# A context tile that arrives already turned, by single-element loads, and tiled matmuls kept together in the plan

## The chip, the core and the metric

The kernel runs on one core of one Trainium2 chip. The metric is the device time of one execution in microseconds. The core has five engines that work from their own instruction queues, each strictly in the order of its queue: PE (TensorE, matrix products and transposes), DVE (VectorE), ACT (ScalarE), POOL (GpSimd) and SP (SyncE, which here only issues transfers). Sixteen DMA engines move the data that SP's and ACT's queues ask for.

## What is computed

Sixteen sequences go through two layers, all in float32. Cut to what matters here, for each sequence `x[b]` (256 tokens of 256 channels), its context `ctx[b]` (256 tokens of 256 channels) and its condition:

```
# layer 0
nx = layer_norm(x) * gamma + beta
scores = (nx @ Wq) @ (ctx @ Wk).T / 16          # 256 x 256
evidence = softmax(scores) @ (ctx @ Wv)
routed = sum over 3 experts of softmax(router)[e] * (silu([nx, evidence, cond] @ e_w1[e]) @ e_w2[e])
x = x + sigmoid(gate) * (routed @ out_w + out_b)
# layer 1: shift, scale and gate of each part come from silu(cond) @ w_ada
x = x + g1 * self_attention(ln(x))               # 16 heads, windows of 128 tokens
x = x + g2 * topk_cross_attention(ln(x), ctx)    # keys and values from ctx, the 16 best of 256 per row
x = x + g3 * swiglu(ln(x))                       # 256 -> 2 x 1024 -> 256
```

So the context is used in three places: as the right side of the evidence scores (channels on the partitions), as the values of the evidence (tokens on the partitions), and as the source of the cross-attention's keys and values (channels on the partitions).

## The kernel before

The kernel is written as a list of small works, and a planner at build time decides the order of the instructions. A work is a generator that yields operations (`Op`): an engine, a cost in microseconds, the buffers that it reads, writes, takes and frees, and a function that emits the instructions. `Flow.run` is a list scheduler: among all operations whose inputs are planned, it takes the one that could begin first by the planner's own costs (`t_mm`, `t_tr`, `t_dve`, `t_act`, `t_pool`; ties and near ties are settled by a rank), emits its instructions, and moves on. The result is one fixed order for each engine. Waits on the chip are set afterwards from the true data dependences between the instructions, not from the plan's times.

`STAGES` lists the stages of a sequence with a rank, the buffers to keep free, a window and the stages that it must follow with a lag in sequences: `evidence` (layer 0 up to the router), `experts`, `self_keys`, `self`, `self_out`, `queries`, `keys`, `cross`, `cross_out`, `inputs`, `mlp`. Several sequences are in work at once, each in another stage.

The tiles that the change touches:

- A sequence's context is loaded as `cx` with tokens on the partitions, by one load of 128 x 2 rows of 1 KB on SP's queue (`sequence`, through the helper `load`, L426).
- `evidence` turns it: `chunks_T` makes four TensorE transposes of 128x128 into a PSUM bank (L484), and `copied` brings the bank to SBUF on ACT or DVE (L518, L520). The turned tile is `cT`.
- `cT` is the right side of the evidence scores (`by_token`, L567), and later the source of `cross_keys`. The planner is told of it as an input of `cross_keys`; for the evidence scores only `qT` is named as an input.
- TensorE works in three ways here: the whole array, `tiled="rows"` (head scores with 16 channels in a strip of 32 rows, L1368 and L1499) and `tiled="columns"` (the weighted sums of heads, L1288, and the router, L1094). The planner charges `TURN` = 0.093 us when the way changes.
- The scaling of the attention weights by GpSimd is `scale` in `self_attention` (L1408), planned with 1.02 us for four pieces.

Of the kernel before, what the change touches and what calls it, by code (L numbers as in the profile page):

```python
# [15 lines left out]
P = 128  # L16
# [20 lines left out]
PE, DVE, ACT, POOL, SP = range(5)  # L37
# [25 lines left out]


def t_pool(cols, n=1):
    return n * (0.03 + cols * 0.00237)


class Buf:
# [26 lines left out]
class Op:  # L96
# [5 lines left out]

    def __init__(
        self, engine, us, trace, r=(), w=(), new=(), free=(), table=None, size=0, tiled=None,
        other=(), grain=0.0,
    ):
        self.grain = grain
        self.tiled = tiled
        self.ways = ((engine, us, trace), *other)
        self.engine, self.us, self.trace, self.table, self.size = engine, us, trace, table, size  # L110
        self.tail = 0.0
        self.r, self.w, self.free = tuple(r), tuple(w), tuple(free)
        self.out = tuple(Buf(ring) for ring in new)
        self.done, self.end = False, 0.0
        self.after = ()
# [10 lines left out]
class Flow:  # L126
# [4 lines left out]
    ASIDE = 1.0  # L131
    TURN = 0.093
    SWITCH = 3.0
    RATE = 0.31e6
    LAND = 1.7

# [95 lines left out]
    def run(self):  # L232
        while self.works:
            moved = False
            for w in tuple(self.works):
                moved |= self.advance(w)
            self.works = [w for w in self.works if w.posted or not w.ended]
            best = None
            for w in self.works:
                wanted = set()  # L240
                for op in w.posted:
                    at = self.start(w, op, wanted)
                    wanted.update(b.ring for b in op.out)
                    if at is None:
                        continue
                    begin = max(self.now[op.engine], at)
                    late = 0.0
                    if op.table and op.table != self.table:
                        late = max(0.0, self.SWITCH - (begin - at))
                    key = (begin + late, at + w.rank + late)  # L250
                    if best is None or key < best[0]:
                        best = (key, w, op, at)
            if best is None:
                if not moved and self.works:
                    raise RuntimeError("no work can go on")
                continue
            _, w, op, at = best
            us = op.us
            begin = max(self.now[op.engine], at)
            if op.table and op.table != self.table:  # L260
                self.table = op.table
                us += self.LOAD
            if op.engine == PE:
                if op.tiled != self.tiled or op.tiled == "rows":
                    us += self.TURN
                self.tiled = op.tiled
            end = begin + us
            if op.grain and op.engine in self.port:
                self.port[op.engine] = begin, end, op.grain
            if op.size:  # L270
                self.moved = max(self.moved, end) + op.size / self.RATE
                op.tail = self.moved + self.LAND - end
            for b in op.out:
                b.ring.take(b)
            op.trace(*(b.t for b in op.out))
            op.done, op.end = True, end + op.tail
            w.posted.remove(op)
            self.now[op.engine] = end
            self.busy[op.engine] += us
            self.log.append((begin, end, op.engine, op.trace))  # L280
            for b in op.out + op.w:
                b.ready, b.by = end + op.tail, op.engine
            for b in op.r + op.w + op.out:
                b.read, b.last = max(b.read, end + op.tail), op.engine
            for b in op.free:
                b.ring.free.append((max(b.read, b.ready) + 0.15, b.slot))
# [3 lines left out]
def pixart_kernel(  # L290
# [9 lines left out]
    nc = tc.nc  # L300
# [63 lines left out]
    units = Ring(tiles(first, FIRST, [P, 2, T], "u"))  # L364
# [45 lines left out]
    flow = Flow()  # L410
# [68 lines left out]
    def chunks_T(src, free=True, ts=ALL):  # L479

        def trace(pt):
            for c in range(2):
                for t in ts:
                    nc.tensor.transpose(  # L484
                        pt[:, c, t * P : (t + 1) * P], src.t[:, t, c * P : (c + 1) * P], ident
                    )
        return (
            yield from make(
                PE, t_tr(2 * len(ts)), trace, r=(src,), new=(banks,),
                free=(src,) if free else (),  # L490
            )
        )
# [22 lines left out]
    def copied(pt):  # L515
        return (
            yield from make(
                ACT, t_copy(512), lambda u: nc.scalar.copy(u, pt.t),  # L518
                r=(pt,), new=(units,), free=(pt,),
                other=((DVE, t_dve(512), lambda u: nc.vector.tensor_copy(u, pt.t)),),  # L520
            )
        )
# [505 lines left out]
    def sequence(b, s):  # L1028
# [11 lines left out]
            3,  # L1040
        )

    def evidence(b, s):
        if "cx" not in s:
            yield from sequence(b, s)
        cx, xb = s["cx"], s["x"]
        pt = yield from chunks_T(cx, free=False)
        cT = s["cT"] = yield from copied(pt)
        xn = yield from normed(xb, 1e-5)
        pt = yield from chunks_T(xn)  # L1050
        nx = yield from by_chunk(
# [8 lines left out]
            r=(sc,), new=(smalls,),  # L1060
        )

        def exps(u):
# [5 lines left out]
        ex = yield from make(  # L1069
            ACT, 0.92, exps, r=(sc,), w=(am,), new=(units,), free=(sc,),  # L1070
            table="exp",
        )
# [231 lines left out]
    def self_weigh(t, v, exs, oT, ended):  # L1304

        pTs = []
        for j in range(4):
            while len(exs) <= j:
                yield None

            def turn(pt, j=j):
                for i in range(4):
                    nc.tensor.transpose(heads4(pt)[:, i, :], heads4(exs[j].t)[:, i, :], ident)  # L1313
            pt = yield from make(PE, t_tr(4), turn, r=(exs[j],), new=(banks,), free=(exs[j],))
            pT = yield from copied(pt)
            pTs.append(pT)

        def sum_up(to):
            for c in range(2):
                for a in range(2):  # L1320
                    for j in range(4):
                        h = 8 * c + 2 * j + a
                        weigh(
                            flat(to), h, c, v.t[:, t, h, :], heads4(pTs[j].t)[:, 2 * c + a, :],
                            a == 0, a == 1,
                        )
        pm = yield from make(
            PE, 1.01, sum_up, r=(v, *pTs), new=(banks,), free=tuple(pTs), tiled="columns",
        )
        yield Op(  # L1330
            ACT, t_copy(256),
            lambda: nc.scalar.copy(
                oT.t[:, :, t * P : (t + 1) * P],
                pm.t[:, 0, :].rearrange("p (c n) -> p c n", c=2),
            ),
            r=(pm,), w=(oT,), free=(pm,),
            other=((DVE, t_dve(256), lambda: nc.vector.tensor_copy(
                oT.t[:, :, t * P : (t + 1) * P],
                pm.t[:, 0, :].rearrange("p (c n) -> p c n", c=2),
            )),),  # L1340
        )
        ended.append(t)
# [15 lines left out]
    def self_attention(b, s, ts):  # L1358
        qT, kM, v = s["self"]
        oT, _, ended = yield from heads(s, v, ts)  # L1360
        for t in ts:
# [19 lines left out]
            for j in range(4):  # L1381
# [23 lines left out]
                def scale(ex=ex, nm=nm):  # L1405
                    for i in range(4):
# [1 line left out]
                        nc.gpsimd.tensor_scalar(  # L1408
                            part, part, nm.t[:, 8 + i : 9 + i], 1.0, ALU.mult, ALU.mult
                        )  # L1410
                yield Op(POOL, 1.02, scale, r=(nm,), w=(ex,), free=(nm,), grain=0.255)
                exs.append(ex)

    def self_output(b, s, ts):
# [8 lines left out]
    def cross_weigh(c, t, v, exs, lefts, oT, ended):  # L1423

        pTs = []
        for j in range(4):
# [3 lines left out]
            def mask_out(s, j=j):  # L1430
# [12 lines left out]
                w=(sm,),  # L1443
# [21 lines left out]
        def sum_up(to):  # L1465
# [7 lines left out]
                        )  # L1473
        pm = yield from make(
            PE, 1.01, sum_up, r=(v, *pTs), new=(banks,), free=tuple(pTs), tiled="columns",
        )
        yield Op(
            ACT, t_copy(128),
# [98 lines left out]
    def mlp(b, s, ts):  # L1577
# [36 lines left out]


    STAGES = (
        ("self_keys", self_keys, 5.0, 2, 2, 4, (("experts", 0), ("self", 1), ("cross", 3))),
        ("evidence", evidence, 5.0, 9, 0, 4, (("experts", 2),)),
        ("self", self_attention, 0.0, 4, 0, 12, (("self_keys", 0), ("cross", 3))),
        ("queries", cross_queries, 3.0, 1, 0, 32, (("self_out", 0), ("cross", 1))),  # L1620
        ("mlp", mlp, 8.0, 4, 0, 6, (("inputs", 0),)),
        ("cross_out", cross_output, 1.0, 1, 0, 8, (("cross", 0),)),
        ("cross", cross_attention, 4.0, 2, 1, 24, (("queries", 0), ("keys", 0))),
        ("experts", experts, 7.0, 3, 0, 8, (("evidence", 0), ("self_out", 3))),
        ("inputs", mlp_inputs, 8.0, 6, 1, 32, (("cross_out", 0), ("queries", 0))),
        ("keys", cross_keys, 6.0, 6, 2, 10, (("evidence", 0), ("cross", 1))),
        ("self_out", self_output, 5.0, 1, 0, 16, (("self", 0),)),
    )
    NEEDS = {
        "self_keys": ("wqkv", "mod"), "self_out": ("wso", "gates"),  # L1630
# [83 lines left out]
```

## Time and profile before

| | us |
|---|---|
| median of 3 runs | 1782.67 (1780.29 to 1784.48) |
| the profiled execution, its own time | 1784.01 |
| its span, first to last instruction | 1782.2 |
| PE busy | 1748.2 (98%) |
| DVE busy | 1406.4 (79%) |
| ACT busy | 1156.4 (65%) |
| POOL busy | 805.5 (45%) |
| transfers of the SP queue, share of 16 DMA engines | 7.8% |

An entry in the profile's groups names the line, the engine, the operation and the tiles (output first, buffer numbers left out), then the count, the busy time, the mean duration and the idle time before it. TensorE's durations overlap, because products are pipelined: a step from start to start is shorter than the duration of one. In float32 each product is run as two passes, so its count in the profile is twice that in the program. DMA rows give the share of 16 engines' time that packets took.

### The profile page before, as it was taken

The numbers are of one execution on the slowest core, as the hardware profiler recorded it, in microseconds if no ns is written. First come the engines' busy times: TensorE is split into PE (matmuls) and PEld (weight loads), VectorE is DVE, ScalarE is ACT, GpSimd is POOL, SyncE is SP. The second block draws the span as 40 slices with busy tenths as digits, with TensorE's granted clock in tenths as the row PEclk, the third lists the DMA queues.
The fourth block names the chain that finished last, engine by engine and source line by source line (L and its number), as shares of the span: only waits on it lengthen the run. The fifth ranks groups of instructions, "written<-read, shape, count | busy, mean of one in ns | idle before, by whom it ended". The sixth has DMA issues, their size and how long they took to land.

```text
span 1782.2 us, 36821 instructions
## 1 busy us (share of the span) xinstructions
PE 1748.2 (98%) x12105; PEld 1416.4 (79%) x12105; DVE 1406.4 (79%) x5637; ACT 1156.4 (65%) x3008; POOL 805.5 (45%) x1809
## 2 busy tenths in 40 slices
PE   8999999999999999999999999999999999999998
PEld 5687878788888788877878787878878787878888
DVE  2223878979988796979899996987986887989982
ACT  3246677776667668585666768577675757685651
POOL 1123355545454545445354554554363635364341
PEclk9999999999999999999999999999999999999999
DMA  8300000000000000000000000000000000010101
GB/s 294 120 18 1 10 16 13 8 13 19 13 19 7 25 13 19 7 25 7 19 13 14 19 8 25 13 15 5 13 19 7 13 19 13 13 37 10 28 31 30
DMA packets 33802, 45.12 MB, mean 25 GB/s; under 512 B 5609, under 2 KB 23579, under 8 KB 33099
## 3 DMA queue, kind: packets, MB, share of 16 engines
q1 hardware_dynamic: 33611, 42.77, 7.8%
q8 instruction: 96, 1.57, 0.4%
q14 instruction: 95, 0.78, 0.1%
HBM read 38.46 MB, written 4.30 MB: 24 GB/s over the span
## 4 chain that ended last, share of the span: by engine, by line
PE 65%; DVE 25%; ACT 4%; issue 2%; POOL 2%; DMA 1%; SPq 0%; POOLq 0%; DVEq 0%; ACTq 0%
PE bank L556 28%; PE bank L567 17%; DVE u L1526 5%; DVE small L1522 4%; PE bank L1457 4%; PE bank L1288 4%; DVE u L1564 3%; DVE small L1557 3%; DVE u L1433 3%; PE bank L1313 3%; PE bank L1499 2%; PE bank L484 2%; PE bank L1368 2%; PE bank L721 1%; ACT u L1393 1%
## 5 line engine op out<-in xcount | busy, mean ns | idle before, releaser
L1449 POOL TENSOR_SCALAR u<-u,small 128x256 f32<-128x256 f32 x512 | 255.2, 514 | 316.8 <-DVE small L1442 281.1
L556 PE MATMUL bank<-u,w 128*128 128x256 f32 x1536 | 360.7, 381 | 0.1
L518 ACT COPY u<-bank 128x512 f32<-128x512 f32 x389 | 222.9, 603 | 190.8 <-PE bank L1457 110.3
L556 PEld LDWEIGHTS bank<-u,w 128*128 128x128 f32 x1536 | 286.2, 191 | 44.2 <-issue 7.4
L1545 ACT ACTIVATE u<-bank,small 128x256 f32<-128x256 f32 x512 | 213.7, 480 | 99.0 <-DVE u L1526 60.7
L556 PE MATMUL bank<-u,wm 128*128 128x256 f32 (+1 forms) x1088 | 248.4, 371 | 3.6 <-ACT u L498 1.9
L1408 POOL TENSOR_SCALAR u<-u,small 128x128 f32<-128x128 f32 x512 | 184.8, 385 | 106.3 <-DVE small L1403 91.3
L1522 DVE MAX8 small<-bank 128x8 f32<-128x256 f32 x512 | 192.6, 418 | 42.4 <-PE bank L1499 42.3
L556 PEld LDWEIGHTS bank<-u,wm 128*128 128x128 f32 x1088 | 189.6, 191 | 35.3 <-issue 6.1
L1526 DVE MATCH_REPLACE8 u<-small,bank 128x256 f32<-128x256 f32 x512 | 208.4, 415 | 0.0
L1433 DVE SCALAR_TENSOR_TENSOR u<-u,u 128x256 f32<-128x256 f32 x512 | 207.6, 446 | 0.0
L1564 DVE MATCH_REPLACE8 u<-small,u 128x256 f32<-128x256 f32 x512 | 205.6, 410 | 0.0
L1557 DVE MAX8 small<-u 128x8 f32<-128x256 f32 x512 | 188.3, 412 | 0.0
L567 PE MATMUL bank<-w,u 128*128 128x256 f32 x768 | 184.3, 383 | 3.8 <-ACT u L498 3.8
L1393 ACT ACTIVATE u<-bank,small 128x128 f32<-128x128 f32 x512 | 180.2, 416 | 10.0 <-DVE small L1384 9.8
L567 PEld LDWEIGHTS bank<-w,u 128*128 128x128 f32 x768 | 142.9, 191 | 25.8 <-ACT u L498 4.9
L1536 POOL TENSOR_SCALAR small<-small 128x2 f32<-128x2 f32 x256 | 55.0, 216 | 222.8 <-DVE small L1522 181.2
L1457 PE MATMUL bank<-ident,u 128*128 128x128 f32 x1024 | 149.9, 276 | 3.9 <-ACT u L498 2.1
L1457 PEld LDWEIGHTS bank<-ident,u 128*128 128x128 f32 x1024 | 121.7, 142 | 35.2 <-POOL u L1449 8.9
L1393 ACT ACTIVATION_READ_ACCUMULATOR u<-bank,small 128x1 f32 x512 | 130.4, 256 | 0.0
L1384 DVE TENSOR_REDUCE small<-bank 128x4 f32<-128x512 f32 x128 | 79.5, 683 | 56.3 <-PE bank L1368 56.2
L596 POOL TENSOR_TENSOR u<-u,u 128x256 f32<-128x256 f32 x96 | 69.8, 748 | 118.1 <-DVE u L588 91.7
(172 smaller groups left out, 3109.0 us busy)
## 6 DMA issues: line engine op xcount, KB each, us to landing
u<-gates_d SPq DMA_DIRECT2D x51, 256.0 KB
u<-in_ctx_dram SPq DMA_DIRECT2D x16, 256.0 KB
w<-in_L_xcond_e_w_dram SPq DMA_DIRECT2D x3, 1024.0 KB
wada<-in_L_xcond_w_ada_dram SPq DMA_DIRECT2D x1, 2304.0 KB
u<-in_x_dram SPq DMA_DIRECT2D x16, 128.0 KB
u<-in_x_dram SPq DMA_DIRECT2D x32, 64.0 KB
wm<-in_L_xcond_w_m_dram SPq DMA_DIRECT2D x1, 2048.0 KB
out_dram<-u SPq DMA_DIRECT2D x16, 128.0 KB
```

The source lines that it names most:

```text
L518: ACT, t_copy(512), lambda u: nc.scalar.copy(u, pt.t),
L556: nc.tensor.matmul(to[:, c, cols(ts)], lhsT=w[:, k, col + c * P : col + (c + 1) * P], rhs=rhs[k // 2].t[:, k % 2, cols(ts)], start=start, ...
L567: nc.tensor.matmul(to[:, t, :], lhsT=lhs[k // 2].t[:, k % 2, t * P : (t + 1) * P], rhs=w(k), start=start, stop=stop,)
L1393: nc.scalar.activation(heads4(u)[:, i, :], heads4(sc.t)[:, i, :], AF.Exp, bias=nm.t[:, i : i + 1], accum_out=nm.t[:, 4 + i : 5 + i],)
L1433: nc.vector.scalar_tensor_tensor(ex[:, a, :], left[:, a, :], TAKEN, ex[:, a, :], ALU.is_equal, ALU.mult, accum_out=s[:, a : a + 1],)
L1449: nc.gpsimd.tensor_scalar(ex, ex, sm.t[:, 2 + a : 3 + a], 1.0, ALU.mult, ALU.mult)
L1457: nc.tensor.transpose(heads4(pt)[:, 2 * a + k, :], exs[j].t[:, a, k * P : (k + 1) * P], ident,)
L1522: nc.vector.max(m8s[j].t[:, 16 * a : 16 * a + 8], sc.t[:, a, :])
L1526: nc.vector.match_replace(firsts[j].t[:, a, :], m8s[j].t[:, 16 * a : 16 * a + 8], sc.t[:, a, :], TAKEN,)
L1545: nc.scalar.activation(u[:, a, :], sc.t[:, a, :], AF.Exp, bias=nm.t[:, a : a + 1])
L1557: nc.vector.max(m8s[j].t[:, 16 * a + 8 : 16 * a + 16], firsts[j].t[:, a, :])
L1564: nc.vector.match_replace(left, m8s[j].t[:, 16 * a + 8 : 16 * a + 16], left, TAKEN)
```

## The change

From the fourth sequence on, a new stage `context` loads the context a second time, with channels on the partitions, straight from DRAM into a tile. It does so by two loads on ACT's queue, one for each half of the channels; partition `p` gets the 256 values `context[b, 0:256, p]`, which lie 1 KB apart in DRAM, so every element is a piece of its own. `evidence` then leaves out the four transposes and the copy. The load with tokens on the partitions stays, since the evidence values need it. The planner counts the operation as 0.2 us of ACT, and its tile as ready 60 us later.

In the planner, `TURN` is charged only between the whole array and either tiled way (before: at any change of way, and at every row-tiled operation). A tiled operation that follows a tiled one is preferred by `STAY` = 2.0 in rank, and the two weighted sums are held back by `HOLD` = 1.0 in rank while the array is whole. GpSimd's costs are raised, and the order of the stages, some ranks, windows and buffers to keep are others.

```diff
 def t_pool(cols, n=1):
-    return n * (0.03 + cols * 0.00237)
+    return n * (0.03 + cols * 0.0027)
...
+    STAY = 2.0
+    HOLD = 1.0
...
-                    key = (begin + late, at + w.rank + late)
+                    rank = w.rank
+                    if op.engine == PE:
+                        if self.tiled is None:
+                            rank += op.hold
+                        elif op.tiled:
+                            rank -= self.STAY
+                    key = (begin + late, at + rank + late)
...
             if op.engine == PE:
-                if op.tiled != self.tiled or op.tiled == "rows":
+                if (op.tiled is None) != (self.tiled is None):
                     us += self.TURN
...
+    def turned_context(b, s):
+
+        if "cx" in s:
+            return
+
+        def trace(t):
+            for c in range(2):
+                nc.scalar.dma_start(
+                    out=t[:, c, :], in_=context[b].rearrange("k (c p) -> c p k", p=P)[c]
+                )
+        op = Op(ACT, 0.2, trace, new=(units,))
+        op.tail = 60.0
+        yield op
+        s["cT"] = op.out[0]
+
     def evidence(b, s):
...
-        pt = yield from chunks_T(cx, free=False)
-        cT = s["cT"] = yield from copied(pt)
+        if "cT" not in s:
+            pt = yield from chunks_T(cx, free=False)
+            s["cT"] = yield from copied(pt)
+        cT = s["cT"]
...
             PE, 1.01, sum_up, r=(v, *pTs), new=(banks,), free=tuple(pTs), tiled="columns",
+            hold=flow.HOLD,
...
-                yield Op(POOL, 1.02, scale, r=(nm,), w=(ex,), free=(nm,), grain=0.255)
+                yield Op(POOL, 1.42, scale, r=(nm,), w=(ex,), free=(nm,), grain=0.355)
...
     STAGES = (
+        ("context", turned_context, 0.0, 8, 0, 4, (("evidence", 1), ("experts", 2))),
         ("self_keys", self_keys, 5.0, 2, 2, 4, (("experts", 0), ("self", 1), ("cross", 3))),
-        ("evidence", evidence, 5.0, 9, 0, 4, (("experts", 2),)),
-        ("self", self_attention, 0.0, 4, 0, 12, (("self_keys", 0), ("cross", 3))),
-        ("queries", cross_queries, 3.0, 1, 0, 32, (("self_out", 0), ("cross", 1))),
+        ("self_out", self_output, 5.0, 1, 1, 16, (("self", 0),)),
+        ("experts", experts, 7.0, 3, 0, 8, (("evidence", 0), ("self_out", 3))),
+        ("queries", cross_queries, 3.0, 1, 0, 4, (("self_out", 0), ("cross", 1))),
...
-        ("inputs", mlp_inputs, 8.0, 6, 1, 32, (("cross_out", 0), ("queries", 0))),
-        ("keys", cross_keys, 6.0, 6, 2, 10, (("evidence", 0), ("cross", 1))),
-        ("self_out", self_output, 5.0, 1, 0, 16, (("self", 0),)),
+        ("self", self_attention, 0.0, 4, 0, 12, (("self_keys", 0), ("cross", 3))),
+        ("inputs", mlp_inputs, 8.0, 8, 1, 24, (("cross_out", 0), ("queries", 0))),
+        ("keys", cross_keys, 4.0, 6, 2, 10, (("evidence", 0), ("cross", 1))),
+        ("evidence", evidence, 5.0, 11, 0, 4, (("experts", 2), ("context", 0))),
     )
```

More of the change, by code (lines that the diff above doesn't have):

```diff
@@ L104, in __init__ @@
         self, engine, us, trace, r=(), w=(), new=(), free=(), table=None, size=0, tiled=None,
-        other=(), grain=0.0,
+        other=(), grain=0.0, hold=0.0,
     ):
+        self.hold = hold
         self.grain = grain
@@ L1475, in cross_weigh @@
             PE, 1.01, sum_up, r=(v, *pTs), new=(banks,), free=tuple(pTs), tiled="columns",
+            hold=flow.HOLD,
         )
@@ L1623, in pixart_kernel @@
         ("cross", cross_attention, 4.0, 2, 1, 24, (("queries", 0), ("keys", 0))),
-        ("experts", experts, 7.0, 3, 0, 8, (("evidence", 0), ("self_out", 3))),
-        ("inputs", mlp_inputs, 8.0, 6, 1, 32, (("cross_out", 0), ("queries", 0))),
-        ("keys", cross_keys, 6.0, 6, 2, 10, (("evidence", 0), ("cross", 1))),
-        ("self_out", self_output, 5.0, 1, 0, 16, (("self", 0),)),
+        ("self", self_attention, 0.0, 4, 0, 12, (("self_keys", 0), ("cross", 3))),
+        ("inputs", mlp_inputs, 8.0, 8, 1, 24, (("cross_out", 0), ("queries", 0))),
+        ("keys", cross_keys, 4.0, 6, 2, 10, (("evidence", 0), ("cross", 1))),
+        ("evidence", evidence, 5.0, 11, 0, 4, (("experts", 2), ("context", 0))),
     )
```

## The prediction

> **What bounds the kernel now.** I read the page's busy row and chain first, then a table of windows through the middle, then the first 80 us, because only there do tiny transfers, a full transfer queue and a resting TensorE occur.
>
> ```profile
> span 1782.2 us, 36821 instructions
> ...
> PE 1748.2 (98%) x12105; PEld 1416.4 (79%) x12105; DVE 1406.4 (79%) x5637; ACT 1156.4 (65%) x3008; POOL 805.5 (45%) x1809
> ...
> PE 65%; DVE 25%; ACT 4%; issue 2%; POOL 2%; DMA 1%; SPq 0%; POOLq 0%; DVEq 0%; ACTq 0%
> ```
>
> ```profile
> 200.00:300.00 100.00, 98.27 (x702) 78.67 (x701) 82.17 (x336) 72.91 (x191) 46.98 (x104) 1.00 0.04 12
> ...
> 900.00:1000.00 100.00, 99.40 (x734) 80.19 (x733) 94.67 (x386) 65.31 (x179) 51.93 (x121) 1.00 0.04 13
> ```
>
> TensorE has no free stretch in the middle (98 to 99% of a window; columns: PE, PEld, DVE, ACT, POOL, clock, DMA share, GB/s), and the DMA engines are 4% used. Whatever TensorE waits for in addition is added to the time; whatever work it loses is taken off.
>
> TensorE's step, from start to start:
>
> ```profile
> 121.25 1.89 PE L556 MATMUL bank<-u,w 128*128 128x256 f32 x8
> 122.97 1.89 PE L567 MATMUL bank<-u,u 128*128 128x256 f32 x8
> ...
> 129.88 0.60 PE L484 MATMUL bank<-ident,u 128*128 128x128 f32 x4
> 130.32 1.89 PE L567 MATMUL bank<-w,u 128*128 128x256 f32 x8
> ```
>
> Eight passes take 1.72 us (215 ns each), four transposes 0.44 us (110 ns each).
>
> Now the only single-element loads of the trace, `bvr` (twice 128x2 elements) on otherwise quiet queues, with the issues behind them, and the windows that hold their packets:
>
> ```profile
> 50.23 0.39 SPq L642 DMA_DIRECT2D bvr<-in_L_xcond_b_qkv_dram  x1
> 51.00 0.39 SPq L642 DMA_DIRECT2D bvr<-in_L_xcond_b_kv_dram  x1
> 51.43 0.98 SPq L642 DMA_DIRECT2D wm<-in_L_xcond_w_m_dram  x2
> 52.51 3.25 SPq L820 DMA_DIRECT2D rb_d<-rbb  x1
> ```
>
> ```profile
> 51.25:51.50 0.25, 0.25 (x3) 0.20 (x2) 0.00 (x0) 0.00 (x0) 0.00 (x0) 1.00 0.17 1
> 51.50:51.75 0.25, 0.25 (x3) 0.22 (x2) 0.00 (x0) 0.00 (x0) 0.00 (x0) 1.00 0.22 2
> 51.75:52.00 0.25, 0.25 (x3) 0.23 (x2) 0.00 (x0) 0.00 (x0) 0.00 (x0) 1.00 0.13 1
> ```
>
> They move 1 to 2 GB/s. The packet records: 272 packets (256 elements, 16 completion writes) in 0.69 us, 450 per us at best, each 7 to 9 ns of an engine. The `rb_d` row shows a second thing: a tiny transfer whose issue normally takes 0.3 us held SP for 3.25 us, because the two `wm` loads before it (80 descriptors for each DMA engine) had not yet gone out.
>
> **The change, part by part.**
>
> *Removed.* Thirteen sequences lose four transposes: 52 x 0.110 = 5.7 us of TensorE, the bound, so -6 us. Thirteen copies of 603 ns (mean of the L518 COPY group) leave ACT or DVE: cover, as both have 20 to 35% to spare.
>
> *Grouping.* In the built order TensorE goes from the whole array to a tiled way 176 times, before 182 times. A step from a whole product into a tiled one is 309 ns in the trace against 216 ns otherwise: 6 x 0.093 = -0.6 us. So this part hardly does what it is named for. GpSimd's costs and the new stage order change the plan alone; the instructions are the same in number, but for six more ACT table loads (168 against 162, 1.28 us each, in ACT's 35% of free time) and some 28 operations moved from DVE to ACT. I bound the reordering by +15 and -15 us (the idle 1 to 2% of the middle windows) and take 0.
>
> *Added.* For each of 13 sequences, 65,536 elements as 2 x 32,768, on 16 engines: 4,098 packets an engine. Its length T decides. Bounds: if the engines alone count, 4,098 x 7 ns = 29 us. If the pace of `bvr` holds, 65,568 / 450 = 146 us. Between these lie the two places where tiny packets had queued up behind larger ones: three `ebr` loads (around 21 to 23 us; best half microsecond 1,094 packets per us, 118 of the 547 being 1 KB rows) give 60 us, and the `rw` load (528 packets of 12 bytes in 0.75 us) gives 93 us. A long load also stands in queues that are full, so I take the middle of these two, T = 75 us, and keep 29 and 146 as ends. Against this stands a rule of the Trainium skill, "DMA: Bandwidth & Descriptors", section "Measured": about 10.5 ns per packet on a small load (measured there on GpSimd's path). That would be 65,568 x 10.5 = 688 us a load, an estimate, and over 8 ms in all; the `bvr` rows, 272 packets in 0.69 us (2.5 ns), decide against it. The same page's "Rules for kernel authors" does speak against this change, and I weigh it as such: a strided last dimension becomes one descriptor per element, and should be rearranged.
>
> *Who waits.* The planner's 60 us delay does not cover the first user: the evidence scores name only `qT` as input. In the built order, TensorE's work between the ACT issue and the score product that reads the tile (L576 there) is, at the steps above, 18, 13, 20, 26, 15, 23, 25, 17, 22, 39, 13, 16 and 26 us: 272 us for 13. The whole program's work counted the same way is 1,653 us for a span of 1,782, so the cover is 272 x 1.08 = 293 us. The score product carries a wait for each of the two loads, TensorE is in order, and behind it stand all other sequences' products; ACT, DVE and POOL run dry within a few us. With 1 us from issue to first packet (`bvr`: 50.23 to 51.25) and 1 us at the end: 13 x 77 - 293 = +708 us.
>
> *ACT's queue.* By the `rb_d` row, the second issue of a pair holds ACT until the first half has gone out, some T/2 = 37 us, and TensorE stops soon for want of emptied banks. That lies inside the same 77 us: after it at most 42 us of TensorE work is left, against 38 us of load. I charge 0; if the cover were all lost to it, +100 us.
>
> *SP's queue.* Transfers of SP and ACT share eight completion semaphores in turn, and a transfer waits for the one eight places earlier. With 12 a sequence, SP's loads behind it wait for the element load, but nearly all come after the score product, which waits for the same. 0.
>
> *The clock.* After TensorE has rested, it comes back at half speed:
>
> ```profile
> 17.00:18.00 1.00, 0.07 (x1) 0.07 (x1) 0.00 (x0) 0.99 (x5) 0.00 (x0) 0.99 1.06 412
> 18.00:19.00 1.00, 1.00 (x2) 0.48 (x3) 0.78 (x3) 0.05 (x1) 0.00 (x0) 0.50 1.04 404
> 19.00:20.00 1.00, 1.00 (x3) 0.48 (x2) 0.00 (x0) 0.00 (x0) 0.00 (x0) 0.50 1.05 401
> 20.00:21.00 1.00, 1.00 (x3) 0.47 (x2) 0.00 (x0) 0.00 (x0) 0.00 (x0) 0.50 1.04 381
> 21.00:22.00 1.00, 1.00 (x3) 0.31 (x2) 0.00 (x0) 0.00 (x0) 0.00 (x0) 0.81 1.23 276
> ```
>
> The clock column: 3.4 us at 0.50, so 1.7 us lost for each stall, 13 x 1.7 = +22 us.
>
> *Given back.* While TensorE stands, DVE and the others finish what they have; some of TensorE's small waits later vanish: -10 us, an estimate from the idle 1 to 2% of the middle.
>
> Sum: 708 + 22 - 6 - 1 - 10 = +713 us on the profiled execution's own 1784.0 us = 2497 us. That execution lies 1.3 us above the median; I state 2495 us.
>
> **The rivals.**
>
> *The descriptors come no faster than for `bvr`* (T = 146 us). For it: the engines were only 0.13 to 0.22 busy then, so something ahead of them set the pace. Against it: only 17 packets an engine, mostly start. 13 x 148 - 293 + 22 - 17 = +1636: 3420 us.
>
> *The DMA engines alone set the pace* (T = 29 us). For it: 7 to 9 ns a packet, and `ebr` packets ran at about that among 1 KB rows. 13 x 31 - 293 + 11 (the one cover of 42 us) = +121, with clock and savings 1920 us.
>
> *The load is covered* (faster). If T stays below the cover, 13 to 42 us and 22 in the mean, TensorE never waits and only -6 us and the planner's ±15 remain: about 1776 us. It decides at T of about 20 us; the packets' own 29 us speak against it.
>
> **How the numbers follow.** Queued pace, T from 45 to about 110 us: 0.55, at 2495. `bvr` pace, T above 110 us: 0.28. Engines alone: 0.14. Covered: 0.03, of it 0.01 for no change. The range 2090 (T = 44) to 3430 (T = 147) leaves out the engine case, the covered case and the tail above. A measurement of this kernel tells 0.2% from no change.
>
> **What would show it.** After: the L576 score product or its weight load has 13 waits on transfers `u<-in_ctx_dram` of 40 to 60 us; ACT's second issue takes some 37 us; PE busy falls to about 70%; the clock row shows half speed after each wait; packets rise by 13 x 65,568 = 852,000. No wait at L576 would prove the length wrong; waits of 125 us the pace; a stall with short transfers the order.

## The result: 15% slower, and below the stated range

| | us |
|---|---|
| before, median of 4 runs beside it | 1783.58 (1780.29 to 1784.55) |
| after, median of 4 runs | 2041.42 (2040.10 to 2043.18) |
| ratio, 95% interval | 1.145 (1.143 to 1.147) |

The change costs 258 us. The direction and the place were forecast; the size was not: 713 us was the likeliest loss, and the range began at 2090 us.

The page of the changed kernel, by the rows that were shown of before, with the clock and DMA rows of the 40 slices and the queue of the new loads (packets, MB, share of 16 engines):

```profile
span 2041.0 us, 36734 instructions
...
PE 1777.0 (87%) x12053; PEld 1442.2 (71%) x12053; DVE 1399.3 (69%) x5609; ACT 1164.0 (57%) x3029; POOL 806.7 (40%) x1809
...
PEclk9998989899897989989898998979889899999999
DMA  8206270530807044090614308070620800000101
...
q10 hardware_dynamic: 852384, 3.41, 25.9%
...
PE 63%; DMA 14%; DVE 11%; ACT 4%; issue 4%; ACTq 3%; POOL 1%; SPq 0%; POOLq 0%; DVEq 0%
```

TensorE fell from 98% to 87%. The clock dips where the DMA row has its bursts, until four fifths of the span: the last load's packets end at 1620 of 2041 us. The chain now holds DMA and ACT's queue with 17% together.

The first load, on ACT and on TensorE (start, duration, engine, line, tiles; in brackets the idle time before and what ended it):

```profile
171.47 19.07 ACTq L1059 DMA_DIRECT2D u<-in_ctx_dram  x2
190.64 0.84 ACT L507 ACTIVATE u<-bank,gb 128x256 f32<-128x256 f32 x2 [18.81 <-issue]
```

```profile
175.75 1.03 PE L576 MATMUL bank<-wso,u 128*128 128x256 f32 x4
191.17 2.07 PE L576 MATMUL bank<-gw,u 128*128 128x256 f32 x4 [14.40 <-ACT u L507]
193.03 3.62 PE L565 MATMUL bank<-u,w 128*128 128x256 f32 x8
...
207.13 0.59 PE L576 MATMUL bank<-u,u 128*128 128x256 f32 x2
212.24 1.22 PE L576 MATMUL bank<-u,u 128*128 128x256 f32 x2 [4.51 <-DMA u<-in_ctx_dram]
```

The two issues hold ACT for 19 us. TensorE works for 5 us more, waits 14.4 us for ACT, comes back with eight passes in 3.4 us where they took 1.7 us before, and at the score product waits another 4.5 us for the tile itself. The second issue ends at 190.54 us, before the first half has landed (its completions come in from 192.16 us on), so ACT does not wait for the data there. After both waits TensorE works at half clock (columns as in the tables of windows above: PE, PEld, DVE, ACT, POOL, clock, DMA share, GB/s):

```profile
190.00:195.00 5.00, 3.83 (x9) 3.12 (x10) 0.00 (x0) 0.84 (x2) 0.00 (x0) 0.50 1.02 7
211.00:213.00 2.00, 0.76 (x2) 0.50 (x2) 0.00 (x0) 0.00 (x0) 0.00 (x0) 0.50 0.00 0
```

The packet records say how long a load is: in the thirteen, 39.4 to 40.9 us from the issue to the last packet, mean 40.1; 65,568 packets at some 1,680 per us, which is 9.5 ns of one of the sixteen engines for each.

### The profile page after: what moved, and what is told of

It reads as the page before. It is cut to its first block, busy times and chain, and to the rows that moved or that the text cites. A ratio compares the mean times of both kernels' runs of the same rounds, so it can differ in the third digit from the quotient of the medians.

```text
span 2041.0 us, 36734 instructions
## 1 busy us (share of the span) xinstructions
PE 1777.0 (87%) x12053; PEld 1442.2 (71%) x12053; DVE 1399.3 (69%) x5609; ACT 1164.0 (57%) x3029; POOL 806.7 (40%) x1809
## 4 chain that ended last, share of the span: by engine, by line
PE 63%; DMA 14%; DVE 11%; ACT 4%; issue 4%; ACTq 3%; POOL 1%; SPq 0%; POOLq 0%; DVEq 0%
PE bank L565 28%; PE bank L576 17%; DMA u<-in_ctx_dram 14%; PE bank L1484 4%; PE bank L1314 4%; ACTq L1059 3%; PE bank L1339 2%; PE bank L1527 2%; DVE u L1554 2%; DVE small L1550 2%; DVE small L1585 1%; PE bank L1395 1%; DVE u L1460 1%; DVE u L1592 1%; PE bank L493 1%
## 5 line engine op out<-in xcount | busy, mean ns | idle before, releaser
L565 PE MATMUL bank<-u,w 128*128 128x256 f32 x1536 | 373.8, 390 | 0.8 <-ACT u L507 0.7
L565 PEld LDWEIGHTS bank<-u,w 128*128 128x128 f32 x1536 | 294.6, 196 | 47.3 <-issue 5.0
L1314 PE MATMUL bank<-u,v 128*32 128x128 f32 x3072 | 107.2, 280 | 43.8 <-ACT u L527 43.8
L1314 PEld LDWEIGHTS bank<-u,v 128*32 128x32 f32 x3072 | 80.8, 111 | 77.9 <-ACT u L527 48.0
```

Of the source, the lines that this page charges most:

```text
L565: nc.tensor.matmul(to[:, c, cols(ts)], lhsT=w[:, k, col + c * P : col + (c + 1) * P], rhs=rhs[k // 2].t[:, k % 2, cols(ts)], start=start, ...
L1314: nc.tensor.matmul(sums[at : at + W, col * P : (col + 1) * P], lhsT=v, rhs=pT, start=start, stop=stop)
```

## The experiments

**Are the loads the whole loss?**

```diff
 def turned_context(b, s):
-        if "cx" in s:
-            return
+        return
```

> The whole change but the element loads: the fourth to sixteenth sequence turn their context by TensorE again, with the new grouping, costs and stage order. If the loads carry the whole loss, this runs within 15 us of the kernel before (1768 to 1798 us). If the new order of stages or the grouping costs something of its own, it is slower by more than that: up to 2041 us if they carry it all.

Measured: 1784.69 us, ratio 1.0016 (1.0007 to 1.0024). The grouping, the costs and the stage order together cost 1 to 4 us; all the rest belongs to the loads.

**Landing or hold?** One issue in place of two, with TensorE's order unchanged:

```diff
-            for c in range(2):
-                nc.scalar.dma_start(
-                    out=t[:, c, :], in_=context[b].rearrange("k (c p) -> c p k", p=P)[c]
-                )
+            nc.scalar.dma_start(
+                out=flat(t), in_=context[b].rearrange("k (c p) -> p (k c)", p=P)
+            )
+            op.out[0].t = flat(t).rearrange("p (k c) -> p c k", c=2)
```

> As the changed kernel, with the same order on TensorE, but each pair of loads is one load of 65,536 elements (the two channel halves interleaved in the tile), so that no second issue stands in ACT's queue. Theory A, the landing decides: the tile still lands 40 us after the issue and the cover is still 18 to 39 us, so the time stays at 2041 us within 15, and the waits move from ACT's consumers to the score product. Theory B, the 18.6 us for which the second issue holds ACT decide: 13 x 15 us go, to about 1850 us.

Measured: 2031.66 us, ratio 1.140 (1.139 to 1.142). The issue's row and TensorE's longest wait (total, times, longest):

```profile
L1058 ACTq DMA_DIRECT2D u<-in_ctx_dram x13: 635/636/755, 174.2 to 1571.6; - x13
```

```profile
PE bank L576 <- DMA u<-in_ctx_dram: 246.3, 13, 29.3
```

ACT is held for 0.64 us instead of 19, yet only 10 us come back. The wait has moved: all thirteen loads now stall the score product, for 19 us each.

**The landing covered, the hold kept.** The planner is told of the first reader:

```diff
-        op.tail = 60.0
+        op.tail = 42.0
...
-        sc = yield from by_token((qT,), lambda k: cT.t[:, k, :], 2, free=(qT,))
+        sc = yield from by_token(
+            (qT,), lambda k: cT.t[:, k, :], 2, free=(qT,), needs=(cT,)
+        )
```

> As the changed kernel, but the planner is told that the evidence scores read the turned context, and that it is ready 42 us after the issue: 42 to 53 us of TensorE work now stand between issue and use. The two issues stay on ACT. Theory A: the wait at the score product goes; what is left is ACT's hold of 18.6 us a pair, of which TensorE can bridge some 4 us, 13 x 14 = 180 us: 1940 to 1980 us. If the hold costs nothing once the landing is covered: about 1780 us. If the wait is not for the landing at all: 2041 us.

Measured: 2001.79 us, ratio 1.123 (1.122 to 1.125), 22 us above the top of what was expected. TensorE's busy row, and its longest waits, which no longer name the load:

```profile
PE 1763.9 (88%) x12053; PEld 1432.2 (72%) x12053; DVE 1404.0 (70%) x5608; ACT 1163.5 (58%) x3028; POOL 809.0 (41%) x1809
```

```profile
PE bank L576 <- ACT u L507: 53.7, 7, 16.9
PE bank L1316 <- ACT u L527: 41.7, 4, 16.0
PE bank L1529 <- ACT u L507: 32.9, 2, 16.7
PE bank L1529 <- ACT u L1361: 16.2, 1, 16.2
```

Waits of 16 to 17 us behind ACT, wherever TensorE happens to be. What the expectation missed is mainly the clock: the same 12,053 passes keep TensorE busy for 1763.9 us, 30 us longer than in the kernel with both mends below, and nothing had been charged for that.

**The hold alone.** The loads are issued and never read:

```diff
-        s["cT"] = op.out[0]
+        s["spare"] = op.out[0]
...
+        if "spare" in s:
+            yield Op(SP, 0.0, lambda: None, free=(s["spare"],))
```

> The changed kernel's two loads a sequence are issued on ACT, but nothing reads their tile: the context is turned by TensorE as in the kernel before. Only the hold of ACT by the second issue is left. Theory: each hold of 18.6 us costs TensorE 14 to 17 us, since it can run ahead only a few us before it wants ACT: 180 to 220 us on 1784.7 us, so 1965 to 2005 us. If the loss of the named-input kernel came from the landing after all: about 1785 to 1800 us.

Measured: 2032.86 us, ratio 1.141 (1.139 to 1.142), so 248 us for loads whose data nobody waits for: 19 us each, the whole hold, and 28 us above the top of what was expected. TensorE's row here, and in the kernel without the loads:

```profile
PE 1782.9 (88%) x12105; PEld 1443.2 (71%) x12105; DVE 1404.1 (69%) x5616; ACT 1144.2 (56%) x3015; POOL 807.9 (40%) x1809
```

```profile
PE 1741.2 (98%) x12105; PEld 1417.9 (80%) x12105; DVE 1407.5 (79%) x5618; ACT 1150.9 (65%) x3017; POOL 810.2 (45%) x1809
```

Their spans are 2031.2 and 1780.9 us. TensorE is idle for 209 us more, 16 us for each hold, as was expected. The same 12,105 passes take 42 us more, at a granted clock of 0.937 in the mean against 0.995. So TensorE bridges a few us of each hold and loses them again to the half clock when it comes back.

**The pair on SP's queue.**

```diff
-                nc.scalar.dma_start(
+                nc.sync.dma_start(
...
-        op = Op(ACT, 0.2, trace, new=(units,))
+        op = Op(SP, 1.0, trace, new=(units,))
```

> As the changed kernel, but the pair of loads is issued on SP's queue, which has room: SP gets to it earlier, so that 26 to 73 us of TensorE work stand between issue and use, and nobody on ACT is held. Theory A: only two loads (cover 26 and 34 us against 40) leave a wait, some 16 us, less 6 us for the transposes: 1780 to 1800 us. If the flood of small packets itself slows the other transfers or SP's held queue starves the gates' loads, it stays above 1850 us.

Measured: 2036.09 us, ratio 1.143 (1.141 to 1.145). This expectation fell. The chain of waits and DVE's longest wait show why:

```profile
PE 61%; DVE 18%; SPq 10%; ACT 5%; DMA 2%; issue 2%; POOL 2%; POOLq 0%; DVEq 0%; ACTq 0%
```

```profile
DVE small L462 <- DMA u<-in_x_dram: 249.1, 13, 29.1
```

The next transfers on SP are the loads of the next sequence's context and `x`. They stand behind the pair:

```profile
227.59 20.16 SPq L1059 DMA_DIRECT2D u<-in_ctx_dram  x2
247.85 18.45 SPq L435 DMA_DIRECT2D u<-in_ctx_dram  x1
266.40 1.61 SPq L435 DMA_DIRECT2D u<-in_x_dram  x3
```

SP is held twice: at the second issue of the pair, and in twelve of thirteen cases for another 18 to 20 us at the plain context load that follows. So `x` is asked for 39 us after the pair began, and the layer norm (L462) that opens `evidence` waits for it thirteen times, 19 us each. The hold was not removed, only handed to another queue.

**Both mends together**, the one issue and the named input, each as in its diff above:

```diff
+            nc.scalar.dma_start(
+                out=flat(t), in_=context[b].rearrange("k (c p) -> p (k c)", p=P)
+            )
...
+        op.tail = 42.0
...
+            (qT,), lambda k: cT.t[:, k, :], 2, free=(qT,), needs=(cT,)
```

> Both mends together on the changed kernel: one load of 65,536 elements on ACT's queue (no second issue behind it) and the planner told of the tile's first reader, ready after 42 us, so that 42 to 53 us of TensorE work stand before the use. Theory: the two costs, landing and hold, are all there is; both gone, the time is that of the kernel without the loads (1784.7 us) less 52 transposes, 1775 to 1795 us. If a long stream of small packets also costs the other transfers or the engines something, it stays above 1800 us.

Measured: 1781.69 us, ratio 1.0004 (0.9996 to 1.0012).

```profile
PE 1734.2 (98%) x12053; PEld 1410.4 (79%) x12053; DVE 1405.1 (79%) x5608; ACT 1162.5 (65%) x3028; POOL 811.0 (46%) x1809
...
PEclk9999999999999999999999999999999999999999
DMA  8301977866909077491919368190919000001001
```

The same 852,000 packets cross the DMA engines, and the time is that of the kernel before: even mended, the change gains nothing that can be told from zero. It is some 3 us below the kernel without the loads, of 6 that the transposes promised, so the small packets themselves cost a few us at most.

This run also splits the loss. The changed kernel's span is 263 us longer (2041.0 against 1777.9 us). TensorE is idle for 220 us of it. The other 43 us are the same 12,053 passes, which take 1777.0 us there and 1734.2 us here. By the clock records, TensorE worked for 106 us at a clock of 0.50 there and for 3 us here.

**Less length.** Same order on TensorE, half the elements, and as in the run with one issue nothing behind the element load (the second half of the score product works on unturned data):

```diff
+            nc.scalar.dma_start(out=t[:, 1, :], in_=context[b, 0:P, :])
+            nc.scalar.dma_start(
+                out=t[:, 0, :], in_=context[b].rearrange("k (c p) -> c p k", p=P)[0]
+            )
```

> The changed kernel with the same order on TensorE, but only the first 128 channels come by single elements; the second half of the tile is filled by one load of plain 1 KB rows (the context's first 128 tokens, unturned, so the second half of the scores' product is of other data), issued first, so that nothing stands behind the element load on ACT. The load is 20 us long against covers of 14 to 42 us (13 to 39 us of TensorE steps times 1.08). Theory, the sum of length less cover: 7 of 13 loads miss by 26 us together, with some 8 us of half clock and 6 us saved: 1800 to 1820 us. If each load cost a fixed sum whatever its length: 2030 us; if in proportion to its elements: 1908 us.

Measured: 1804.04 us, ratio 1.012 (1.010 to 1.014).

```profile
PE bank L576 <- DMA u<-in_ctx_dram: 33.6, 8, 10.0
```

A load half as long costs 22 us, where the one issue of full length cost 249: the cover absorbs the rest. Eight loads miss their cover, by 34 us together; seven and 26 us were expected from the counted covers.

**The pace by itself.** A kernel with nothing but element loads, one after the other, of `n` tokens and one half of the channels, and then both halves on two queues:

```python
def turned(c, n, queue):
    queue.dma_start(
        out=got[:, c, 0:n], in_=context[0, 0:n].rearrange("k (c p) -> c p k", p=P)[c]
    )
...
for n in (2, 4, 8, 16, 32, 64, 128, 256):
    turned(0, n, nc.scalar)
    step()
for c, queue in ((0, nc.scalar), (1, nc.sync)):
    turned(c, 256, queue)
```

> Nothing of the computation: one core loads 128 x n single elements of the context, n = 2, 4, 8, ... 256, each after the last has landed, and then the two 128 x 256 halves at once, one on ACT's and one on SP's queue; the outputs are filled with the sum of what was loaded. Theory A, a start of some 0.5 us and then the engines' own pace: the 2-element load runs at about 400 packets per us as in the trace before, and the pace climbs with n to 1,690 per us; the two halves at once take the same 38 us as one after the other. Theory B, the pace depends on the source's pattern: the 2-element load of the context already runs near 1,690 per us. Theory C, the pace is that of one queue: the two halves at once take 19 us.

The DMA issues of that run, from issue to landing in the last column (median us where there are several):

```profile
got<-in_ctx_dram SPq DMA_DIRECT2D x1, 128.0 KB, 40.3
got<-in_ctx_dram ACTq DMA_DIRECT2D x1, 64.0 KB, 11.3
got<-in_ctx_dram ACTq DMA_DIRECT2D x1, 32.0 KB, 6.6
got<-in_ctx_dram ACTq DMA_DIRECT2D x1, 1.0 KB, 2.1
got<-in_ctx_dram ACTq DMA_DIRECT2D x1, 2.0 KB, 2.3
got<-in_ctx_dram ACTq DMA_DIRECT2D x1, 4.0 KB, 2.5
```

From 32 to 64 KB, 8,192 more elements take 4.7 us: 0.57 ns each over all engines. What lies under it is a fixed 2 us. By the packet records the rate is 362, 590, 940, 1,425, 1,484, 1,632, 1,667 and 1,664 packets per us for 2 to 256 elements a partition: theory A. The two halves at once, one on each queue, took 37.9 us from first to last packet, against 19.7 us for one half alone. The pace belongs to something that both queues share, not to one queue.

**The old order with the mended load.** The edit is on the kernel before: its stage list, costs and grouping stay, and the load comes in with one issue and the named input.

```diff
+            nc.scalar.dma_start(
+                out=flat(t), in_=context[b].rearrange("k (c p) -> p (k c)", p=P)
+            )
...
+        op.tail = 42.0
...
+            (qT,), lambda k: cT.t[:, k, :], 2, free=(qT,), needs=(cT,)
...
+        ("context", turned_context, 0.0, 8, 0, 4, (("evidence", 1), ("experts", 2))),
-        ("evidence", evidence, 5.0, 9, 0, 4, (("experts", 2),)),
+        ("evidence", evidence, 5.0, 9, 0, 4, (("experts", 2), ("context", 0))),
```

> The kernel before, with its own order of stages and planner's costs, and only the turned context added in its mended form: one load on ACT's queue, the first reader named, ready after 42 us. Theory: the load is hidden, 52 transposes of 0.11 us and 13 copies go: 1772 to 1790 us, as for the mended changed kernel. If the old order has less room between issue and use than planned, it lies above 1800 us.

Measured: 1868.07 us, ratio 1.048 (1.047 to 1.050): a miss, and not by the load's waits. Two windows of this kernel (busy time and instructions of PE, PEld, DVE, ACT and POOL, then the clock, the DMA share and GB/s):

```profile
1100.00:1500.00 400.00, 397.36 (x2712) 326.03 (x2711) 289.15 (x1148) 255.13 (x677) 180.00 (x399) 1.00 0.51 17
1500.00:1866.00 366.00, 312.83 (x2192) 237.46 (x2190) 325.04 (x1388) 202.56 (x530) 162.46 (x358) 0.89 0.06 16
```

The first of them in the kernel before:

```profile
1100.00:1500.00 400.00, 396.70 (x2803) 321.43 (x2802) 332.52 (x1333) 272.88 (x727) 200.74 (x446) 1.00 0.05 14
```

While the loads run (DMA share 0.51) TensorE is 99% busy. The last one is issued at 1328 us. After 1500 us TensorE is idle for 53 of 366 us and its clock falls to 0.89, while DVE is busy for 325. The plan that came out of the old stage list has left DVE's work to the end: from 100 to 1500 us it holds 87 us less of it than the plan of the kernel before, and 43 of these are in the window shown. That DVE then holds TensorE up is read from these rows and was not tried, nor was another lag for the new stage.

## Why the prediction was wrong, point by point

- *The bound, the place, the sign.* Right. TensorE had no room, the score product did not have its tile, and ACT was held by the second issue.
- *T, the length of a load, is the step that failed.* "I take the middle of these two, T = 75 us": it is 40. With 41 us from issue to use, the prediction's own sum is 13 x 41 - 293 + 1 (for the one cover of 42 us) + 22 - 6 - 1 - 10 = +246 us, 2030 us where 2041 were measured. The error lay in reading a steady pace off short or mixed transfers. The 272 packets of `bvr` in 0.69 us were nearly all start: in the pace run 272 packets take 0.75 us, and 528 take 0.89. In the `ebr` half microsecond the 118 rows of 1 KB took 59 ns each by their records, two thirds of the packet time. Its 429 elements took 9.0 ns each, and 4,098 x 9.0 is 37 us.
- *"A long load also stands in queues that are full"*, the reason for the middle, fell with it. In the pace run's load of 256 tokens an engine gets a packet every 9.6 ns, and a packet's own record is 8.8 ns in the mean. By these records the engines worked nearly all the time, which leaves little room for something ahead of them that set the pace. The rival with the engines alone had the mechanism, at a chance of 0.14, and was low because it took 7 ns, the lower end of the records. (Its 1920 us leaves out the 10 us given back; with them its terms make 1910.)
- *The cover of 293 us.* Right. With one issue the score product waits 246 us in all; 13 x 41 - 293 = 240. With half the elements 34 us, where 26 were counted.
- *ACT's hold at 0, at most +100 us.* Its length, T/2, was right (18.6 us in the mean for T = 40). In the changed kernel its addition to the landing is small: 2041.42 against 2031.66 with it gone. But alone it costs 217 us (named input) or 248 us (unread loads), so the bound of 100 was wrong. The two waits overlap: each by itself brings nearly the whole loss, and taking one away brings back 10 or 40 us.
- *SP at 0.* Held for the changed kernel: 17 of SP's issues fell into a load there, and none took over 0.6 us. With the trial on SP, where SP's own issues were held, this shows that the hold stays within a queue.
- *Half clock after a stall.* Right in kind, half the size: 22 us were charged and 43 came (1777.0 against 1734.2 us for the same passes). The charge was for one stop a load, and with one issue it fits (1756.3 us, so 22). The changed kernel makes 20 stops of over 3 us for 13 loads. The idle time was charged with 231 us and is 220, so that the two errors partly cancel in the 2030 us above.
- *Grouping and order, 0 within 15 us.* Right: +2.4 us between the medians. *Transposes, -6 us*: some 3 us were seen, between two kernels of different order.

## What to carry to other kernels

Price a long transfer from the difference between two sizes, and never from the rate of a short one: start-up filled the short one here, and cost the forecast a factor of two in the length of the load. Before moving a transfer to a quiet queue, look at what stands next on that queue: here an issue right behind a load of 32,768 elements was held for 18 to 21 us, and all that stood after it with it. And when two waits overlap, taking one away shows little; only the run without either shows what they cost.

## What the runs showed of the hardware that was not expected

- A single issue of 65,536 elements took ACT 0.64 us; two issues of 32,768 took it 19 us. It is the next transfer on the same queue that waits.
- An element of 4 bytes costs an engine 9.5 ns in a long load, 0.6 ns over all sixteen, and a second queue adds only from 1,664 to 1,729 packets per us.
- With both waits gone, a stream of elements that ran for 510 of 1778 us slowed the kernel by no more than a few us (ratio 1.0004).
- A stop of TensorE costs more than its length: with the unread loads the return at a clock of 0.50 added 3 us for each hold (42 us over thirteen).
